# Second moments of 64-channel groups: one 128-column product per chunk half, or two 64-column products in the two halves of the array's columns

## The chip, the cores and the metric

The kernel runs on one core of one Trainium2 chip. The metric is the time of one execution on the device, in microseconds (us); lower is better. All tensors are float32.

The names used for the engines are those of the profile: PE is TensorE's matrix products and PEld its loads of weights (the stationary operand), DVE is VectorE, ACT is ScalarE, POOL is GpSimd, SP is SyncE, which here only issues DMAs.

## The reference

Two layers. The first computes 49 attention weights for every pixel from a dilated 7x7 convolution, a 1x1 convolution and a softmax, and sums the 49 shifted inputs with these weights. The second whitens the result in groups of 64 channels, and this is where the second moments come from:

```python
def _L1_conv_ref(X, weight, bias):
    NUM_CHANNELS = 64
    ...
    nc = NUM_CHANNELS
    g = C // nc
    x = jnp.transpose(X, (1, 0, 2, 3)).reshape(g, nc, -1)
    m = x.shape[-1]
    mean = x.mean(-1, keepdims=True)
    xc = x - mean
    I = jnp.broadcast_to(jnp.eye(nc, dtype=X.dtype), (g, nc, nc))
    Sigma = EPS * I + jnp.einsum('gdm,gem->gde', xc, xc) / m
    rTr = (1.0 / jnp.einsum('gii->g', Sigma))[:, None, None]
    Sigma_N = Sigma * rTr
    P = I
    for _ in range(T_ITERS):
        P3 = jnp.einsum('gij,gjk,gkl->gil', P, P, P)
        P = 1.5 * P - 0.5 * jnp.einsum('gij,gjk->gik', P3, Sigma_N)
    wm = P * jnp.sqrt(rTr)
    xn = jnp.einsum('gde,gem->gdm', wm, xc)
    X_hat = jnp.transpose(xn.reshape(C, B, H, W), (1, 0, 2, 3))
    return X_hat * weight + bias
```

The input is 4 images of 256 channels and 64x64 pixels, so there are four groups of 64 channels, and only the 64x64 blocks on the diagonal of the channel-by-channel moments are wanted.

## The kernel before

**Layout.** Channels lie on the partitions, 128 at a time (`NCC` = 2 halves, index `cc`). An image is split by the parity of rows and columns into four phases, so there are 16 phases `n` in all, and a phase is cut into 8 chunks of 128 pixels. Two phases share a slot in SBUF; the attention's result overwrites the input there.

**The convolution.** It is a fast algorithm with 7 evaluation points in each direction. `conv_bank` (L411, products at L430) multiplies a 49-column stationary operand with a moving operand of 128 or 162 columns; the inner loop `h` puts the two column phases into the partitions from 0 and from 64 of the same PSUM bank, so that it uses the array's columns in two halves. A row of evaluation points takes 104 products.

**The attention.** `softmax` (L565) turns the logits by the array (L571), takes the softmax on DVE and ACT, and stores the weights from the tile `zt` to DRAM by 8 DMAs of SP (L607). `load_band` (L616) reads them back skewed (L619), DVE transposes them into `band` (L630), `make_block` (L638) transposes a chunk of the input (L644, copied out at L651), and `weighted_sum` (L662) multiplies it with pieces of `band` of 64 to 352 columns (L676). `store_y` writes the result to the slot with ACT (L690).

**The second moments.** For each of the 128 chunks, `turn_y` (L700) transposes the result (two 128x128 products at L705) and ACT copies it from PSUM into one of three tiles `yt` (L712), which hold 128 channels and a column of ones for each half. `moments` (L714) then multiplies, for each half, the 128 channels as stationary operand with the 129 columns as moving operand (L718), and adds all chunks up in the PSUM tile `sig`: 128 columns of products and one column of sums. Of each 128x128 block the two off-diagonal quarters belong to no group; L877 sets them to zero with the mask `blk` at the end.

**The end.** After the last chunk, DVE forms the means `mu` (L866) and the scaled moments `S` (L872) from `sig`, a chain of small products gives the whitening matrices (L868 to L922), and a last pass multiplies all pixels with them (L937) and stores the output.

**What sets the order.** PE executes its products in the order of the program text, since `pe` keeps them so; the other engines' orders are made by a scheduler when the program is built. Of the eight calls of `moments` in a phase, four lie in `second_half` (L778) and four in `finish` (L746). Around them lie transposes (L644, L705) and weighted sums (L676); the call for chunk 3 is followed by the next step of the convolution wherever one is left. The convolution of image b+1 runs beside the attention of image b, so PE alternates between the two.

Of the kernel before, what the change touches and what calls it, by code (L numbers as in the profile page):

```python
# [8 lines left out]
F32 = mybir.dt.float32  # L9
AF = mybir.ActivationFunctionType  # L10
ALU = mybir.AluOpType
# [19 lines left out]
def kernel(  # L31
# [29 lines left out]
    nc = tc.nc  # L61
    B, C, H, W = x.shape
    P = 128
    NCC = C // P
# [6 lines left out]
    NCH = SH // CR  # L71
    HALF = SH // 2
    NPIX = B * H * W
    GW = 64
# [18 lines left out]
    def pe(ins):  # L93
        return tc.keep_in_program_order(ins)
# [7 lines left out]
    ps_sg = ctx.enter_context(tc.tile_pool(name="ps_sg", bufs=1, space=bass.MemoryType.PSUM))  # L102

    def tp():
        return ps_tp.tile([P, 512], F32, tag="tp", name="tp")
# [50 lines left out]
    t = tp()  # L156
# [3 lines left out]
    t = tp()  # L160
# [5 lines left out]
    for k in range(2):  # L166
        t = ps_cv.tile([P, 512], F32, name=f"cv{k}")
        nc.vector.memset(t, 0.0)
        cv_buf.append(t)
    sig = ps_sg.tile([P, NCC, P + 1], F32, name="sig")  # L170

# [366 lines left out]
    bpool = ctx.enter_context(tc.tile_pool(name="bp", bufs=1, side="right"))  # L540
# [5 lines left out]
    NY = 3  # L546
    yt_buf = []
    for k in range(NY):
        a = bpool.tile([P, NCC, P + 1], F32, name=f"yt{k}")
        nc.gpsimd.memset(a, 1.0)  # L550
        yt_buf.append(a)
    sd = []
    ND = SH + 2 * R
    for k in range(4):
        t = dram.tile([ND * DR], F32, name=f"sd{k}")
# [78 lines left out]
    def where(n):  # L634

        return slots[n // 2], n % 2
# [60 lines left out]
    count = [0]  # L697
    ybs = {}

    def turn_y(n, i):  # L700
        yt, pc = where(n)
        t = tp()
        for cc in range(NCC):
            pe(
                nc.tensor.transpose(  # L705
                    t[:, cc * P : (cc + 1) * P],
                    yt[:, cc, CR * i : CR * (i + 1), bass.ds(pc, SW, 2)],
                    ident,
                )
            )  # L710
        yb = ybs[n, i] = yt_buf[len(ybs) % NY]
        nc.scalar.copy(yb[:, :, :P], t[:, :C].rearrange("p (a c) -> p a c", a=NCC))  # L712

    def moments(n, i):  # L714
        yb = ybs[n, i]
        for cc in range(NCC):
            pe(
                nc.tensor.matmul(  # L718
                    sig[:, cc],
                    yb[:, cc, :P],  # L720
                    yb[:, cc, :],
                    start=(count[0] == 0 and cc == 0),
                    stop=(count[0] == 4 * B * NCH - 1),
                    skip_group_check=True,
                )
            )
        count[0] += 1

    spill = {}
# [16 lines left out]
    def finish(last=True):  # L746

        n = open_n[0]
        turn_y(n, 4)
        turn_y(n, 5)  # L750
        moments(n, 4)
        turn_y(n, 6)
        moments(n, 5)
        turn_y(n, 7)
        moments(n, 6)
        if n % 2:
            move(n // 2)
        if last:
            moments(open_n.pop(), 7)
# [90 lines left out]
    for k in range(3):  # L850
        t = rpool.tile([P, NCC, SH, W], F32, name=f"back{k}")
# [7 lines left out]
    def square(name):  # L859
        return bpool.tile([P, P], F32, tag="xb", name=name, bufs=5)  # L860

    wm, sc, beta = [], [], []
    for cc in range(NCC):
        G = sig[:, cc]
        mu = work.tile([P, 1], F32, tag="mu", name=f"mu{cc}")
        nc.vector.tensor_scalar(mu, G[:, P : P + 1], 1.0 / NPIX, None, ALU.mult)  # L866
        t = tp()
        nc.tensor.matmul(t[:1, :P], mu, ident, start=True, stop=True)  # L868
        row = work.tile([1, P], F32, tag="row", name=f"row{cc}", bufs=1)
        nc.vector.tensor_copy(row, t[:1, :P])  # L870
        S = work.tile([P, P], F32, tag="S", name=f"S{cc}")
        nc.vector.tensor_scalar(S, G[:, :P], 1.0 / NPIX, None, ALU.mult)  # L872
        t = tp()
        nc.tensor.matmul(t[:, :P], row, row, start=True, stop=True)
        nc.vector.tensor_tensor(S, S, t[:, :P], ALU.subtract)
        nc.vector.scalar_tensor_tensor(S, ident, EPS, S, ALU.mult, ALU.add)
        nc.vector.tensor_tensor(S, S, blk, ALU.mult)  # L877
        dt_ = square(f"dt{cc}")
        nc.vector.tensor_tensor(dt_, S, ident, ALU.mult)
        dg = work.tile([P, 1], F32, tag="dg", name=f"dg{cc}")  # L880
        nc.vector.tensor_reduce(dg, dt_, AX.X, ALU.add)
        t = tp()
        nc.tensor.matmul(t[:, :1], blk, dg, start=True, stop=True)
        rtr = work.tile([P, 1], F32, tag="rtr", name=f"rtr{cc}")
        nc.vector.reciprocal(rtr, t[:, :1])
        nc.vector.tensor_scalar(S, S, rtr, None, ALU.mult)


        Pm = square(f"P{cc}_0")
        nc.vector.tensor_scalar(Pm, ident, 1.5, None, ALU.mult)  # L890
        nc.vector.scalar_tensor_tensor(Pm, S, -0.5, Pm, ALU.mult, ALU.add)
        for it in range(1, T_ITERS):
            t = tp()
            nc.tensor.matmul(t[:, :P], Pm, Pm, start=True, stop=True)
            P2 = square(f"P2_{cc}_{it}")
            nc.vector.tensor_copy(P2, t[:, :P])
            t = tp()
            nc.tensor.matmul(t[:, :P], P2, Pm, start=True, stop=True)  # L898
            P3 = square(f"P3_{cc}_{it}")
            nc.vector.tensor_copy(P3, t[:, :P])  # L900
            t = tp()
            nc.tensor.matmul(t[:, :P], P3, S, start=True, stop=True)  # L902
            Pn = square(f"P{cc}_{it}")
            nc.vector.tensor_scalar(Pn, Pm, 1.5, None, ALU.mult)
            nc.vector.scalar_tensor_tensor(Pn, t[:, :P], -0.5, Pn, ALU.mult, ALU.add)
            Pm = Pn


        q = work.tile([P, 1], F32, tag="q", name=f"q{cc}")
        nc.scalar.activation(q, rtr, AF.Sqrt)  # L910
        qi = work.tile([P, 1], F32, tag="qi", name=f"qi{cc}")
        nc.vector.reciprocal(qi, q)
        nc.vector.scalar_tensor_tensor(q, qi, rtr, q, ALU.mult, ALU.add)
        scale = work.tile([P, 1], F32, tag="scale", name=f"scale{cc}")
        nc.vector.scalar_tensor_tensor(
            scale, q, 0.5, gain_sb[:, cc : cc + 1], ALU.mult, ALU.mult
        )
        t = tp()
        nc.tensor.matmul(t[:, :1], Pm, mu, start=True, stop=True)
        bt = work.tile([P, 1], F32, tag="beta", name=f"beta{cc}")  # L920
        nc.vector.tensor_scalar(bt, t[:, :1], scale, -1.0, ALU.mult, ALU.mult)
        nc.vector.tensor_tensor(bt, bt, shift_sb[:, cc : cc + 1], ALU.add)  # L922
        wm.append(Pm)
        sc.append(scale)
        beta.append(bt)
# [5 lines left out]
    for b in (3, 2, 1, 0):  # L931
        for cc in range(NCC):
            for q in range(SH // TR):
                st = rpool.tile([P, TR, 2, W], F32, tag="out", name=f"out_{b}_{cc}_{q}", bufs=4)
                for pr in range(2):
                    t = tp()
# [6 lines left out]
                        start=True,  # L943
                        stop=True,
# [46 lines left out]
```

## Time and profile before

| | us |
|---|---|
| median of 3 runs | 991.78 |
| lowest and highest of them | 989.21, 992.46 |
| the profiled execution | 991.09 |
| its span, first to last instruction | 989.3 |
| PE busy in the span | 793.0 |
| PEld busy | 694.3 |
| DVE busy | 660.3 |
| ACT busy | 305.2 |

The spans of busy time of different engines overlap. A float32 product appears in the trace as two weight loads and two matrix products, so the 256 products of `moments` are 512 records on PE and 512 on PEld. [...] what counts in a dense stretch is the distance from start to start. The first moments come at 301.0 us, the last at 887.2 us of the span.

### The profile page before, as it was taken

Reading aid. Unit: us, or ns where it says so; the run is one execution under the profiler, and the core shown is the slowest. Engines: PE = TensorE matmul, PEld = TensorE weight load, DVE = VectorE, ACT = ScalarE, POOL = GpSimd, SP = SyncE. Lnnn points to the kernel's source line nnn. Section 1 sums busy time; section 2 is a strip of 40 time slices with the busy share of each in tenths; the row PEclk is TensorE's granted clock in tenths of the full one; section 3 lists DMA queues with packets and bytes.
Section 4 is the critical chain, followed back from the end, with each engine's and each line's share of the span. In section 5 each row is a group of like instructions: output and inputs, shape, how many; then the busy total and the mean of one; then the engine's idle time right before and its main releaser. Section 6 shows DMA issues by size and latency. Waiting matters only on the chain.

```text
span 989.3 us, 19053 instructions
## 1 busy us (share of the span) xinstructions
PE 793.0 (80%) x7739; PEld 694.3 (70%) x7739; DVE 660.3 (67%) x1469; ACT 305.2 (31%) x654; POOL 38.1 (4%) x50
## 2 busy tenths in 40 slices
PE   5995575752679999894999989589997678885898
PEld 5995575752668889794888979578896557663443
DVE  3006999999996885998489589979567311113344
ACT  1214222331223333332243434213323323330143
POOL 2102000030000010001001000000000000000000
PEclk9988787877779999997899999989998879995699
DMA  9737221136575363269718223953214972200277
GB/s 277 176 64 190 89 71 62 55 106 230 97 154 127 109 186 90 59 171 192 155 46 247 74 66 86 166 119 100 56 45 132 246 116 51 48 0 1 85 309 286
DMA packets 189711, 122.09 MB, mean 123 GB/s; under 512 B 139655, under 2 KB 180664, under 8 KB 188600
## 3 DMA queue, kind: packets, MB, share of 16 engines
q1 hardware_dynamic: 184600, 90.73, 36.7%
q0 software_dynamic: 5024, 30.15, 9.9%
q8 instruction: 61, 1.00, 0.4%
q14 instruction: 26, 0.21, 0.1%
HBM read 69.64 MB, written 51.21 MB: 122 GB/s over the span
## 4 chain that ended last, share of the span: by engine, by line
PE 52%; DVE 9%; ACT 4%; DMA 3%; SPq 3%; issue 3%; DVEq 0%; ACTq 0%
PE cv L430 20%; PE y L676 15%; PE tp L937 6%; PE sig L718 4%; SPq L607 2%; PE tp L644 2%; DMA band<-sd 2%; PE tp L705 2%; DVE band L630 1%; DVE pv L282 1%; ACT slot L690 1%; ACT pv L439 1%; DVE zz L282 1%; PE tp L898 1%; PE tp L902 1%
## 5 line engine op out<-in xcount | busy, mean ns | idle before, releaser
L430 PE MATMUL cv<-xh,wr 128*49 128x128 f32 (+1 forms) x5408 | 335.3, 287 | 61.7 <-DVE xh L275 50.3
L430 PEld LDWEIGHTS cv<-xh,wr 128*49 128x49 f32 x5408 | 324.1, 128 | 69.8 <-issue 63.8
L676 PE MATMUL y<-band,xb 128*128 128x352 f32 (+5 forms) x768 | 178.1, 375 | 62.0 <-DVE band L630 45.5
L676 PEld LDWEIGHTS y<-band,xb 128*128 128x128 f32 x768 | 124.4, 206 | 82.2 <-issue 40.8
L630 DVE STREAM_TRANSPOSE band<-band 128x1408 f32<-128x1408 f32 x32 | 50.6, 1619 | 60.8 <-DMA band<-sd 60.8
L718 PE MATMUL sig<-yt 128*128 128x129 f32 x512 | 82.1, 283 | 11.2 <-ACT yt L712 11.1
L651 ACT COPY xb<-tp 128x256 f32<-128x256 f32 x128 | 46.0, 373 | 129.8 <-PE tp L644 129.5
L718 PEld LDWEIGHTS sig<-yt 128*128 128x128 f32 x512 | 71.3, 195 | 17.3 <-ACT yt L712 14.6
L439 ACT COPY pv<-cv 113x486 f32<-113x486 f32 (+1 forms) x84 | 39.8, 474 | 116.2 <-PE cv L430 113.4
L690 ACT ACTIVATE slot<-y,pivot 128x512 f32<-128x512 f32 x64 | 42.5, 721 | 64.3 <-PE y L676 64.3
L705 PE MATMUL tp<-ident,slot 128*128 128x128 f32 x256 | 52.9, 299 | 10.0 <-ACT slot L690 9.0
L282 DVE SCALAR_TENSOR_TENSOR xh<-ct 128x512 f32<-128x512 f32 x56 | 36.7, 683 | 30.2 <-PE cv L430 30.2
L712 ACT COPY yt<-tp 128x256 f32<-128x256 f32 x128 | 45.2, 378 | 33.7 <-PE tp L705 33.5
L644 PEld LDWEIGHTS tp<-ident,slot 128*128 128x128 f32 x256 | 44.3, 205 | 15.2 <-issue 6.3
L644 PE MATMUL tp<-ident,slot 128*128 128x128 f32 x256 | 52.7, 303 | 2.3 <-DVE d L581 2.3
L275 DVE TENSOR_TENSOR ct<-rb 128x1024 f32<-128x1024 f32 x28 | 33.9, 1211 | 29.8 <-ACT rb L361 29.6
L705 PEld LDWEIGHTS tp<-ident,slot 128*128 128x128 f32 x256 | 39.4, 204 | 17.4 <-ACT slot L690 14.0
L282 DVE SCALAR_TENSOR_TENSOR pv<-pv 113x162 f32<-113x162 f32 x168 | 49.0, 318 | 0.1
L233 PE MATMUL tp<-w2c,w 128*128 128x245 f32 x196 | 47.6, 409 | 0.0
L952 DVE TENSOR_SCALAR out<-tp,scale,beta 128x512 f32<-128x512 f32 x32 | 25.9, 810 | 32.5 <-PE tp L937 32.5
L233 PEld LDWEIGHTS tp<-w2c,w 128*128 128x128 f32 x196 | 45.7, 314 | 1.4
L282 DVE SCALAR_TENSOR_TENSOR xh<-rb 128x512 f32<-128x512 f32 x28 | 19.2, 686 | 37.5 <-PE cv L430 37.5
(152 smaller groups left out, 899.8 us busy)
## 6 DMA issues: line engine op xcount, KB each, us to landing
wr<-gd SPq DMA_DIRECT2D x108, 196.0 KB, 2.7
out_dram<-out SPq DMA_DIRECT2D x32, 512.0 KB, 2.6
sd<-zt SPq DMA_DIRECT2D x128, 112.0 KB, 2.8
band<-sd SPq DMA_DIRECT2D x64, 224.0 KB, 4.0
slot<-in_x_dram POOLq DMA_DIRECT2D x12, 1024.0 KB, 12.0
gd<-wr SPq DMA_DIRECT2D x36, 196.0 KB, 2.0
w<-in_L_conv_w_dram SPq DMA_DIRECT2D x2, 3136.0 KB, 12.1
spill<-slot POOLq DMA_DIRECT2D x3, 2048.0 KB, 10.4
```

What stands on the lines that cost most here:

```text
L233: nc.tensor.matmul(t[:, : MID * KT], tap(cc, a, s, v), w2c[:, a].rearrange("p b k -> p (b k)"), start=(a == 0), stop=(a == na - 1),)
L282: return STT(o, a, f, b, ALU.mult, ALU.add)
L430: nc.tensor.matmul(cv[h * HB : h * HB + KT, k, sr : sr + n, sc : sc + n], wv[:, sc, sr, cc], xh[bc][:, :n, h * NCC + cc, :n], start=(j == ...
L439: nc.scalar.copy(pvs[b, br][:K2, i0 : i0 + len(pts)].rearrange("p n q b -> p (n q b)"), cv[:K2, : len(pts)].rearrange("p n q b two -> p (n ...
L630: nc.vector.transpose(f, f)
L644: nc.tensor.transpose(t[:, cc * P : (cc + 1) * P], xt[:, cc, CR * m : CR * (m + 1), bass.ds(pc, SW, 2)], ident,)
L651: nc.scalar.copy(xb, t[:, :C])
L676: nc.tensor.matmul(ps[:, cc, q0 - half * HALF : q1 - half * HALF, :], xb[:, cc * P : (cc + 1) * P], rhs, start=(k == 0), stop=(k == len(PI ...
L690: nc.scalar.activation(yt[:, cc, half * HALF : (half + 1) * HALF, bass.ds(pc, SW, 2)], ps[:, cc], AF.Identity, bias=pivot[:, cc : cc + 1],)
L705: nc.tensor.transpose(t[:, cc * P : (cc + 1) * P], yt[:, cc, CR * i : CR * (i + 1), bass.ds(pc, SW, 2)], ident,)
L718: nc.tensor.matmul(sig[:, cc], yb[:, cc, :P], yb[:, cc, :], start=(count[0] == 0 and cc == 0), stop=(count[0] == 4 * B * NCH - 1), skip_gr ...
L937: nc.tensor.matmul(t, wm[cc], slots[2 * b + pr][:, cc, q * TR : (q + 1) * TR, :].rearrange("p r w -> p (r w)"), start=True, stop=True,)
```

## The change

Each product of `moments` over 128 channels becomes two, one for each group of 64. A group's 64 channels are the stationary operand, and the same 64 channels with their own column of ones are the moving operand (65 columns). The first group's result goes to partitions 0 to 63 of `sig`, the second's to 64 to 127, in the same columns, so the two products use the two halves of the array's columns. `sig` and `yt` get the shapes that this needs, `turn_y` copies four runs of 64 channels instead of two of 128, and at the end `S` is cleared and its two diagonal blocks are filled one by one.

```diff
-    sig = ps_sg.tile([P, NCC, P + 1], F32, name="sig")
+    sig = ps_sg.tile([P, NCC, GW + 1], F32, name="sig")
...
-        a = bpool.tile([P, NCC, P + 1], F32, name=f"yt{k}")
+        a = bpool.tile([P, NCC, P // GW, GW + 1], F32, name=f"yt{k}")
...
-        nc.scalar.copy(yb[:, :, :P], t[:, :C].rearrange("p (a c) -> p a c", a=NCC))
+        nc.scalar.copy(
+            yb.rearrange("p a g c -> p (a g) c")[:, :, :GW],
+            t[:, :C].rearrange("p (e c) -> p e c", c=GW),
+        )
...
         for cc in range(NCC):
-            pe(
-                nc.tensor.matmul(
-                    sig[:, cc],
-                    yb[:, cc, :P],
-                    yb[:, cc, :],
-                    start=(count[0] == 0 and cc == 0),
-                    stop=(count[0] == 4 * B * NCH - 1),
-                    skip_group_check=True,
+            for g in range(P // GW):
+                pe(
+                    nc.tensor.matmul(
+                        sig[g * GW : (g + 1) * GW, cc],
+                        yb[:, cc, g, :GW],
+                        yb[:, cc, g],
+                        start=(count[0] == 0 and cc == 0),
+                        stop=(count[0] == 4 * B * NCH - 1),
+                        skip_group_check=True,
+                    )
                 )
-            )
...
-        nc.vector.tensor_scalar(mu, G[:, P : P + 1], 1.0 / NPIX, None, ALU.mult)
+        nc.vector.tensor_scalar(mu, G[:, GW : GW + 1], 1.0 / NPIX, None, ALU.mult)
...
-        nc.vector.tensor_scalar(S, G[:, :P], 1.0 / NPIX, None, ALU.mult)
+        nc.vector.memset(S, 0.0)
+        for g in range(P // GW):
+            gs = slice(g * GW, (g + 1) * GW)
+            nc.vector.tensor_scalar(S[gs, gs], G[gs, :GW], 1.0 / NPIX, None, ALU.mult)
```

In the built programs, the order of PE's instructions is the same but for the products of `moments`: four products in place of two for each chunk. On the other engines the scheduler moved a few neighbours past each other. Two of them lie near DMAs: in the third and fourth image, SP's load of the convolution weights of row 1, bank 5 (L297) stands behind the first eight stores of attention weights (L607) instead of ahead of them. The two clearings of `S` stand at the very start of DVE's order.

## The prediction

> **What bounds the kernel now.** I read the page first (busy shares, then the chain that ended last), then the groups by form, then the chain in ten windows between 295 and 900 us, where all moments lie, and last the timeline of PE around single calls of `moments`.
>
> ```profile
> PE 793.0 (80%) x7739; PEld 694.3 (70%) x7739; DVE 660.3 (67%) x1469; ACT 305.2 (31%) x654; POOL 38.1 (4%) x50
> ...
> PE 52%; DVE 9%; ACT 4%; DMA 3%; SPq 3%; issue 3%; DVEq 0%; ACTq 0%
> PE cv L430 20%; PE y L676 15%; PE tp L937 6%; PE sig L718 4%; SPq L607 2%; PE tp L644 2%; DMA band<-sd 2%; PE tp L705 2%; DVE band L630 1%; DVE pv L282 1%; ACT slot L690 1%; ACT pv L439 1%; DVE zz L282 1%; PE tp L898 1%; PE tp L902 1%
> ```
>
> PE is the busiest engine and carries most of the chain. L718, the moments, has 4% of it. In the ten windows I counted 92 chain pieces of L718, 41 us in all, which are 93 of the 128 calls. So what a call gains or loses on PE shows in the end for some 7 calls in 10; the others lie where PE afterwards waits for ACT (L690) or for `band`.
>
> ```profile
> L430 PEld LDWEIGHTS cv<-xh,wr 128*49 128x49 f32 x5408 | 324.1, 128 | 69.8 <-issue 63.8 <-ACT pv L439 1.1
> L430 PE MATMUL cv<-xh,wr 128*49 128x128 f32 x4624 | 305.4, 282 | 0.0
> ...
> L718 PE MATMUL sig<-yt 128*128 128x129 f32 x512 | 82.1, 283 | 11.2 <-ACT yt L712 11.1
> L718 PEld LDWEIGHTS sig<-yt 128*128 128x128 f32 x512 | 71.3, 195 | 17.3 <-ACT yt L712 14.6
> ```
>
> The convolution, L430, is the model for the new products: it already puts 49-column weights into the two halves of the columns. Its 5408 records fill little more than 300 us, although one lasts 282 ns: they overlap. The timeline gives the distances:
>
> ```profile
> 425.83 12.14 PE L430 MATMUL cv<-xh,wr 128*49 128x162 f32 x208
> ```
>
> ```profile
> 484.52 1.24 PE L676 MATMUL y<-band,xb 128*128 128x320 f32 x4
> 485.60 0.61 PE L718 MATMUL sig<-yt 128*128 128x129 f32 x4
> 486.14 1.04 PE L430 MATMUL cv<-xh,wr 128*49 128x162 f32 x14
> ```
>
> ```profile
> 498.00 0.28 PE L430 MATMUL cv<-xh,wr 128*49 128x128 f32 x2
> ...
> 498.21 0.75 PE L705 MATMUL tp<-ident,slot 128*128 128x128 f32 x4
> ...
> 500.56 0.61 PE L718 MATMUL sig<-yt 128*128 128x129 f32 x4
> ...
> 501.01 0.40 PE L705 MATMUL tp<-ident,slot 128*128 128x128 f32 x2
> ...
> 501.74 0.64 PE L644 MATMUL tp<-ident,slot 128*128 128x128 f32 x4
> ```
>
> Columns: start in us, length in us, engine, line, operation, and how many records were merged. Four things are to be seen. (1) A call between full-width products takes 501.01 - 500.56 = 0.45 us: four records, 0.112 each. (2) The convolution's 208 records take 12.14 us, less 0.28 for the last one's passage, so a pair of records takes 11.86 / 104 = 0.114 us: two halves for the price of one full-width record. (3) Before a convolution the same call takes 486.14 - 485.60 = 0.54, so going from full width into halves costs 0.09. (4) Coming back, the first transposes start 0.21 after the last pair, whose own stream takes 0.11: 0.10 lost; and the four of them then take 0.75 where they take 0.64 in a dense stretch (501.74): another 0.11, a full-width weight load that could not be made ahead.
>
> [...] In the trace a full-width load follows the last at 0.11[...]. [...]
>
> **The change, part by part.**
>
> *The stream of a call.* Before: 4 records at 0.112, 0.45 us. After: 8 records, 4 pairs. A pair's columns are 65 instead of 129, and its weights 64 instead of 128, so it should take half of 0.112: 0.056; 4 x 0.057 = 0.23. A gain of 0.22. Bounds: with pairs that overlap imperfectly, five slots instead of four, 0.29; with no overlap at all (64 columns per load, one after the other) 0.45, no gain. I take 0.23, since L430's pairs do overlap.
>
> *The switches.* Before, a call lies in full-width work. Now it begins with a switch into halves, 0.09, and its first weight load of 64 columns is exposed, 0.05. It ends with a switch back. No row shows that for 65 columns: the loss is 0.10 if it begins when the stream ends, and 0.15 if the 0.21 from start to start is fixed (0.21 - 0.06). I take 0.12. Then the next product's full-width load is exposed, 0.11 (498.21 against 501.74). Sum: 0.37 lost, 0.22 gained: a call with full-width neighbours is longer by 0.15 (0.12 to 0.18).
>
> *By neighbours, on the chain.* I took each call's predecessor and successor from the timeline. 61 of the 93 have full-width work right before and after: 61 x 0.145 = +8.8 us. Ten go over into the convolution: there the switch existed, and it only moves to the call's front; the exit is free. Eight of them gain the 0.22 and lose nothing but a little weight load, 8 x -0.20 = -1.6; two also begin after a wait, [...] the exposed load shrinks from 0.11 to 0.05: 2 x -0.40 = -0.8. Eight others begin after a wait for `yt` (L712) and end in full-width work: 0.11 + 0.45 before, 0.05 + 0.23 + 0.12 + 0.11 after, -0.05 each, -0.4. The rest are calls that wait inside for `yt` (33 calls are stretched so, by 0.05 to 0.10); the longer call before them eats that wait: about eight on the chain, -0.5.
>
> *Off the chain.* 32 of the other 35 calls lie between full-width products, + 4.6 us of PE time there. It is covered by PE's waits, such as the half microsecond before L705 that waits for ACT L690. A fifth may come through: +1.0 (0 to 3).
>
> *SP's order.* In images 3 and 4 a weight load of the convolution no longer stands ahead of eight stores.
>
> ```profile
> 438.01 0.32 SPq L297
> ...
> 438.38 0.43 SPq L607
> ```
>
> That load waits for the end of the convolution (438.0), and the stores behind it are on the chain. `zt` was written by 437.90 (L598, 437.34 and 0.56 long), so they can start 0.4 earlier: 2 x -0.4 = -0.9 with its issue. The load itself is needed only at 486, and comes out at about 444.
>
> *Small edits.* The `yt` copy moves the same 128x256 in four runs; L651's contiguous one takes 373 ns, this one with two runs 378, so 5 ns more at most. The two clearings of `S` lie at the start of DVE, under PE's wait for weights (7 us); without that cover 0.3 us. Two fills of 64 columns instead of one of 128 (280 ns) stand in DVE's queue ahead of the second `mu`, and partly ahead of nothing that is waited for: the row copy (L870, 888.27) waits for PE anyway. Zero, at most 0.2. DVE's and ACT's other swaps: between -1 and +2, taken as 0.
>
> Sum: 8.8 - 1.6 - 0.8 - 0.4 - 0.5 + 1.0 - 0.9 = +5.6 us. On the profiled execution's own 991.09 that is 996.7; the median is 0.7 above it, so 997.
>
> **Rivals.**
>
> *No overlap of the short pairs.* Each call loses 0.22 more: the gain is gone and the switches stay. About 80 chain calls x 0.22 = +18: 1015. For it: the pair is so short that each half's load and stream have to fit into 0.056 us, and nothing in this trace is that short. Against: L430's pairs start together everywhere. 0.08.
>
> *The switches are mostly absorbed.* If the exit costs 0.10 and a longer call eats more of the `yt` and ACT waits than I counted, a call loses 0.10 and some 15 of the 61 vanish: +2 in sum, 994. For it: DVE and SP hold a good part of the chain between 430 and 470 and again from 620 to 650. Against: the second half of a phase is PE back to back. 0.22.
>
> *No switch at all, faster.* If what I read as a switch belongs to the convolution alone (its semaphores, its 162-column start), 64-column products flow between full-width ones, and each of the 93 calls saves 0.22: -20 us, 971. Place: entry and exit of `moments`. The point is 0.22 us for both together; below it the change gains. For it: all switches in this trace have the convolution on one side. Against: the entry into L430 costs the same 0.09 after L718 and after L676, the exit the same 0.10 before L644 and L705, whose weights lie ready in both cases. 0.08, together with smaller gains by luck of the order.
>
> **How the numbers follow.** The forecast has 0.62. Its own range: the exit (-1.5 to +1.8), five slots for four (+4.5), off the chain (-1 to +2), the other engines' order (-1 to +2): 994 to 1004. A measurement of this kernel tells about 0.3% from no change, 3 us. The absorbed case lies within it, as does the low end of my own; the case without overlap adds to slower. Slower 0.71, within 0.3% 0.20, faster 0.09. With half of the absorbed case taken in, the range is 992 to 1005.
>
> **What would show it.** In the profile after: L722, the new products, with 1024 records; a call from first start to the next product's start near 0.39 with 0.23 of it in four pairs (a pair near 0.057); the transposes behind it 0.1 longer; calls before the convolution shorter by 0.2; PE's busy time nearly the same; L718's 4% of the chain not smaller. The stores of `zt` in images 3 and 4 should no longer follow the load at the convolution's end. I am wrong if a call with its switches takes less than 0.45, or if PE's added time doesn't reach the chain.

## The result, and the profile after

| | before | changed |
|---|---|---|
| median, us | 990.5 (4 runs) | 995.79 (4 runs) |
| lowest and highest, us | 988.54, 992.46 | 995.47, 996.29 |
| profiled execution, us | 991.09 | 996.29 |
| span of it, us | 989.3 | 994.5 |

The ratio of changed to before is 1.0054, 95% interval 1.003 to 1.0078: slower by 5.3 us (3.0 to 7.7). The forecast was 997, 0.5% above the 991.78 that was the median of before then.

The page of the changed kernel, its busy line and its chain:

```profile
PE 801.3 (81%) x8251; PEld 677.6 (68%) x8251; DVE 661.4 (67%) x1473; ACT 305.3 (31%) x654; POOL 38.1 (4%) x50
...
PE 52%; DVE 9%; ACT 4%; DMA 3%; SPq 3%; issue 3%; DVEq 0%; ACTq 0%
PE cv L430 19%; PE y L676 16%; PE tp L944 6%; PE sig L722 3%; PE tp L705 3%; SPq L607 3%; PE tp L644 2%; DMA band<-sd 2%; DVE band L630 1%; ACT slot L690 1%; ACT pv L439 1%; DVE pv L282 1%; DMA sd<-zt 1%; DVE zz L282 1%; DVE xh L282 1%
```

The costliest groups of the changed kernel (busy us, mean ns of one, idle time before):

```profile
L705 PE MATMUL tp<-ident,slot 128*128 128x128 f32 x256 | 59.2, 324 | 10.2 <-ACT slot L690 9.3
L722 PE MATMUL sig<-yt 128*64 128x65 f32 x1024 | 58.2, 235 | 9.4 <-ACT yt L712 8.9
```

The same transposes in the kernel before:

```profile
L705 PE MATMUL tp<-ident,slot 128*128 128x128 f32 x256 | 52.9, 299 | 10.0 <-ACT slot L690 9.0
```

The moments themselves became cheaper: L722 is busy for 58.2 us where L718 was for 82.1, and its share of the chain falls from 4% to 3%. But the transposes behind them, L705, rose from 52.9 to 59.2 us although their code is the same, and all of PE from 793.0 to 801.3. Each single call shows it. The timeline of PE around two calls between full-width work, that is, between products that use all 128 columns of the array (start, length, engine, line, operation, records merged):

```profile
500.37 0.45 PE L722 MATMUL sig<-yt 128*64 128x65 f32 x8
500.76 0.51 PE L705 MATMUL tp<-ident,slot 128*128 128x128 f32 x2
501.19 0.45 PE L722 MATMUL sig<-yt 128*64 128x65 f32 x8
501.57 0.74 PE L644 MATMUL tp<-ident,slot 128*128 128x128 f32 x4
```

The same place in the kernel before:

```profile
500.33 0.40 PE L705 MATMUL tp<-ident,slot 128*128 128x128 f32 x2
500.56 0.61 PE L718 MATMUL sig<-yt 128*128 128x129 f32 x4
501.01 0.40 PE L705 MATMUL tp<-ident,slot 128*128 128x128 f32 x2
501.25 0.66 PE L718 MATMUL sig<-yt 128*128 128x129 f32 x4
```

And the changed kernel around the call ahead of a convolution:

```profile
484.41 1.34 PE L676 MATMUL y<-band,xb 128*128 128x320 f32 x4
485.68 0.45 PE L722 MATMUL sig<-yt 128*64 128x65 f32 x8
485.96 1.22 PE L430 MATMUL cv<-xh,wr 128*49 128x162 f32 x18
```

From first start to the next product's start a call takes 500.76 - 500.37 = 0.39 us, 0.06 less than before. Against this, the two transposes take 0.51 instead of 0.40, and the call starts 501.19 - 500.76 = 0.43 after them where it started 0.24 after (501.01 and 501.25). From one call to the next the kernel before repeats every 0.69 us (500.56 to 501.25), the changed one every 0.82 (500.37 to 501.19): 0.13 longer. Ahead of a convolution the call takes 0.28 instead of 0.54. The weight loads show where a part of this lies: before, they start 0.11 to 0.12 us ahead of their product (500.90 for the transposes at 501.01, 500.44 for the call at 500.56); in the changed kernel those of the call start with it, both at 500.37, and those of the transposes behind it at 500.75 and 500.76. A load that starts with its product is the exposed load of the prediction.

### The profile page after: what moved, and what is told of

Its sections match the earlier page's. It is cut to its first block, busy times and chain, and to the rows that moved or that the text cites. A ratio compares the mean times of both kernels' runs of the same rounds, so it can differ in the third digit from the quotient of the medians.

```text
span 994.5 us, 20076 instructions
## 1 busy us (share of the span) xinstructions
PE 801.3 (81%) x8251; PEld 677.6 (68%) x8251; DVE 661.4 (67%) x1473; ACT 305.3 (31%) x654; POOL 38.1 (4%) x50
## 4 chain that ended last, share of the span: by engine, by line
PE 52%; DVE 9%; ACT 4%; DMA 3%; SPq 3%; issue 3%; DVEq 0%; ACTq 0%
PE cv L430 19%; PE y L676 16%; PE tp L944 6%; PE sig L722 3%; PE tp L705 3%; SPq L607 3%; PE tp L644 2%; DMA band<-sd 2%; DVE band L630 1%; ACT slot L690 1%; ACT pv L439 1%; DVE pv L282 1%; DMA sd<-zt 1%; DVE zz L282 1%; DVE xh L282 1%
## 5 line engine op out<-in xcount | busy, mean ns | idle before, releaser
L676 PE MATMUL y<-band,xb 128*128 128x352 f32 (+5 forms) x768 | 183.1, 382 | 64.7 <-DVE band L630 47.2
L676 PEld LDWEIGHTS y<-band,xb 128*128 128x128 f32 x768 | 125.7, 207 | 86.6 <-DVE band L630 37.1
L705 PE MATMUL tp<-ident,slot 128*128 128x128 f32 x256 | 59.2, 324 | 10.2 <-ACT slot L690 9.3
L722 PE MATMUL sig<-yt 128*64 128x65 f32 x1024 | 58.2, 235 | 9.4 <-ACT yt L712 8.9
L722 PEld LDWEIGHTS sig<-yt 128*64 128x64 f32 x1024 | 40.4, 137 | 33.7 <-ACT yt L712 13.2
L644 PE MATMUL tp<-ident,slot 128*128 128x128 f32 x256 | 55.5, 314 | 0.0
L705 PEld LDWEIGHTS tp<-ident,slot 128*128 128x128 f32 x256 | 39.1, 206 | 21.7 <-ACT slot L690 14.0
```

The source lines that it names most:

```text
L644: nc.tensor.transpose(t[:, cc * P : (cc + 1) * P], xt[:, cc, CR * m : CR * (m + 1), bass.ds(pc, SW, 2)], ident,)
L676: nc.tensor.matmul(ps[:, cc, q0 - half * HALF : q1 - half * HALF, :], xb[:, cc * P : (cc + 1) * P], rhs, start=(k == 0), stop=(k == len(PI ...
L705: nc.tensor.transpose(t[:, cc * P : (cc + 1) * P], yt[:, cc, CR * i : CR * (i + 1), bass.ds(pc, SW, 2)], ident,)
L722: nc.tensor.matmul(sig[g * GW : (g + 1) * GW, cc], yb[:, cc, g, :GW], yb[:, cc, g], start=(count[0] == 0 and cc == 0), stop=(count[0] == 4 ...
```

## The experiments

Each was run beside the kernel before on the same chip, whose median there was 991.8 to 992.1 us.

| run | median, us | ratio to before, 95% interval |
|---|---|---|
| e1 full width, small edits kept | 990.91 | 0.9989 (0.9977 to 1.0001) |
| e2 before, one load on POOL | 989.1 | 0.9972 (0.9963 to 0.998) |
| e3 halves, four calls together | 980.7 | 0.9893 (0.9874 to 0.9912) |
| e4 full width, four calls together | 990.53 | 0.9992 (0.9978 to 1.0006) |
| e5 before, an extra visit to the halves | 1017.27 | 1.0259 (1.0245 to 1.0273) |
| e6 changed, loops swapped | 996.5 | 1.0045 (1.0031 to 1.0059) |
| e7 changed, the same load on POOL | 998.49 | 1.0065 (1.0052 to 1.0079) |
| e8 halves, batch ahead of the sum | 980.51 | 0.9883 (0.9867 to 0.99) |
| e9 full width, batch ahead of the sum | 988.11 | 0.9963 (0.9949 to 0.9978) |

**e1: only the halves undone.**

```diff
-            for g in range(P // GW):
-                ... sig[g * GW : (g + 1) * GW, cc], yb[:, cc, g, :GW], yb[:, cc, g]
+            ... sig[:, cc], yb[:, cc, :P], yb[:, cc, :]
...
-            nc.vector.tensor_scalar(S[gs, gs], G[gs, :GW], 1.0 / NPIX, None, ALU.mult)
+            nc.vector.tensor_scalar(S[gs, gs], G[gs, gs], 1.0 / NPIX, None, ALU.mult)
```

> The change without its halves: products of 128 by 129 columns as before, but the copy into yt in four runs, S cleared and filled block by block, and mu from column 128. Theory (the halves and their switches make the loss): as the kernel before, 988 to 993 us. Rival (the small edits make it: the copy, the fills of S): as the changed kernel, 994 us or more.

990.91 us, no difference from before. The four-run copy, the cleared `S` and its two fills cost nothing that can be measured; the loss comes with the 64-column products and with what the scheduler made of them.

**e5: a visit to the halves by itself.** Two 64x65 products, whose results nothing reads, stand ahead of each call of the kernel before.

```diff
+        for g in range(P // GW):
+            pe(nc.tensor.matmul(extra[g * GW : (g + 1) * GW],
+                                yb[:, 0, g * GW : (g + 1) * GW], yb[:, 0, : GW + 1], ...))
         for cc in range(NCC):
```

> The kernel before, with two 64 by 65 products in the column halves put ahead of each call of moments, into unused columns of the bank of sig; nothing is taken away. It measures a visit to the halves by itself. Theory: entry 0.09, exposed load 0.05, two pairs 0.12, exit 0.09 beyond the stream, exposed full-width load 0.10: 0.45 us a visit, for some 93 calls on the chain 40 us: 1028 to 1034. Rival (the switch belongs to the convolution alone): two pairs only, 0.12 x 93 = 11: 1003.

The timeline of PE in e5 around one such call (L707 are the transposes, L720 the extra products, L731 the moments):

```profile
511.26 0.40 PE L707 MATMUL tp<-ident,slot 128*128 128x128 f32 x2
511.59 0.34 PE L720 MATMUL sig<-yt 128*64 128x65 f32 x4
511.86 0.71 PE L731 MATMUL sig<-yt 128*128 128x129 f32 x4
512.41 0.40 PE L707 MATMUL tp<-ident,slot 128*128 128x128 f32 x2
```

From transposes to transposes it is 1.15 us where it was 0.68 (500.33 to 501.01), so a visit costs 0.47 us: the price was right (0.45 expected), and the convolution has no part in it. But the whole is 25 us longer, not 36 to 42. A part of the reason is found in the weighted sums, below.

**e3 and e4: four calls together.** The four calls of a half phase are made at its end, with six `yt` tiles, so that four calls share the switches; e4 does the same with the full-width products.

```diff
-    NY = 3
+    NY = 6
...
+    def four(n, h):
+        for i in range(4 * h, 4 * h + 4):
+            moments(n, i)
...
-        moments(n, 0)
...
-        moments(n, 3)
+        four(n, 0)
```

> The changed products, but the four calls of moments of a half phase together at its end (six yt tiles in place of three), so that there is one entry into halves and at most one exit per four calls. Theory (stream 0.23 us a call, 0.14 for the entry, 0.23 to 0.26 for the exit, free where a convolution follows): 32 batches of 1.06 plus some 16 exits make 38 us of PE where before has 58, some 70% of it on the chain: 977 us, 972 to 984, faster than both kernels. Rival (the short pairs bring nothing that shows): not below 988.

> The same batching with the full-width products of before: what the moving alone does. Theory: the products take as long as before, so 990 us, give or take 5 for transposes that now wait for their copies with less to fill the wait; 10 to 18 us above the batched halves. Rival (batching itself is the gain): within 3 us of the batched halves.

A batch of e3 on PE, and the same batch in e4:

```profile
480.35 1.15 PE L722 MATMUL sig<-yt 128*64 128x65 f32 x32
481.33 1.44 PE L430 MATMUL cv<-xh,wr 128*49 128x162 f32 x21
```

```profile
482.37 1.95 PE L718 MATMUL sig<-yt 128*128 128x129 f32 x16
484.25 2.98 PE L430 MATMUL cv<-xh,wr 128*49 128x162 f32 x48
```

The busy lines of their pages, e3 first:

```profile
PE 772.8 (79%) x8251; PEld 667.9 (68%) x8251; DVE 661.8 (68%) x1473; ACT 300.7 (31%) x654; POOL 38.9 (4%) x53
```

```profile
PE 794.0 (80%) x7739; PEld 694.3 (70%) x7739; DVE 660.6 (67%) x1469; ACT 300.6 (30%) x654; POOL 38.9 (4%) x53
```

Four calls take 481.33 - 480.35 = 0.98 us in halves and 484.25 - 482.37 = 1.88 in full width. This batch goes over into the convolution; where full-width work follows, a batch in halves takes 1.08. e3 is 11 us faster than before and some 15 us faster than the changed kernel, with the same 64-column products; e4, with the same moves, is no faster than before. So the products in halves are worth having, and what made the change lose is the number of visits: one for each call.

SP's order is not the same in all of these: e3 has that of the changed kernel, and e4 has one load more behind the stores, so what e3 gains over the kernel before can hold something of the 2.8 us of e2, below. e8 and e9, further below, both have the order of the kernel before, and there the halves are 7.6 us ahead.

**e6: the loops swapped.**

```diff
-        for cc in range(NCC):
-            for g in range(P // GW):
+        for g in range(P // GW):
+            for cc in range(NCC):
```

> The changed kernel with its two loops swapped: both halves of the channels for the first group, then both for the second, so that products of the same columns follow each other. If only products in different columns overlap: a call's stream is three slots of a single record longer or more, 0.06 to 0.22 us, 5 to 18 us in all: 1001 to 1014. If the array takes records as they come, two at a time: as the changed kernel, 996.

996.5 us, as the changed kernel. A call on PE in e6, and then one in the changed kernel:

```profile
300.93 0.46 PE L722 MATMUL sig<-yt 128*64 128x65 f32 x8
301.31 0.51 PE L705 MATMUL tp<-ident,slot 128*128 128x128 f32 x2
```

```profile
301.37 0.45 PE L722 MATMUL sig<-yt 128*64 128x65 f32 x8
301.76 0.51 PE L705 MATMUL tp<-ident,slot 128*128 128x128 f32 x2
```

0.38 against 0.39 here, and 0.390 against 0.383 in the mean of the calls between full-width work: the products of the two halves need not alternate in the program. In the trace the records still start in pairs, only 13 ns apart instead of 7. A record does not name its half, so which two run side by side is not shown.

**e2 and e7: SP's order.** The load of the convolution weights of row 1, bank 5 in images 3 and 4 is issued by POOL, in the kernel before (e2) and in the changed one (e7), so that SP's order is the same in the two.

```diff
-                nc.sync.dma_start(w[bc], gd[br]...)
+                q = nc.gpsimd if (b > 1 and br == 1 and i == 2) else nc.sync
+                q.dma_start(w[bc], gd[br]...)
```

> The kernel before, with only the load of weights of row 1, bank 5 in images 3 and 4 issued by POOL, so that SP's stores of attention weights need not stand behind it. The prediction took 0.9 us for the same move in the changed kernel: 989.6 us. The trace after points to more: the drift against before falls by some 2 us at each of the two places, which would give 986 to 987. If the drift falls for another reason, no change: 990.5.

> The changed kernel with the load of row 1, bank 5 in images 3 and 4 issued by POOL, as in the run of before with it there. With SP's order the same in both, what stays between the two is the moments. Theory (the order hid part of what the halves cost): as the changed kernel, 995 to 997, so 6 to 8 us above the kernel before with the load on POOL (989.1). Rival (the order has no part): 993, the same 3 us lower as before was.

e2 is faster by 2.8 us (2.0 to 3.7), three times what I had taken for this order and less than the 3.5 to 4.5 that I then read from the trace. In the changed kernel, which has it by the scheduler, the chain of waits at the first of the two places reads:

```profile
438.64 0.48 DVE zt L598
439.12 0.12 DVE s L590
439.24 0.28 SPq L607
```

The stores (L607) now follow the tile that they store (L598). Before, they followed the load (L297), which follows the convolution's end on PE. That cuts PE's delay off from them: measured by the starts of the same products, the changed kernel is 2.1 us behind at 428 and 0.8 behind at 469, where the next weighted sum starts; at the second place it goes from 2.5 behind at 607 to 0.7 behind at 648. (It is 0.3 ahead at 481, but the rest of that is the sum itself, which ran at a higher granted clock than before, 0.74 against 0.63.) I had priced the wait (0.4 us each), not that PE's lost time no longer runs through this chain. With the order the same in both, e7 stands 1.0065 / 0.9972 = 0.93% above e2, 9 us (7 to 12 by the ends of the two intervals): that is what the 64-column products bring, with all that they set off. It is not their price alone: in the two profiled executions, 7.8 us apart, 2.8 us arise between 619 and 648 us, where only four calls lie. What causes that is not shown. e7 itself came out at 998.5, neither at 995 to 997 nor at 993; its interval and that of the changed kernel overlap.

**The weighted sums and the granted clock.** The 24 records of a phase's first weighted sum (L676, with the transposes between them) take 4.8 us from the first start to the last in some phases and 6.3 to 7.8 in others, in every kernel. Three windows, each around the same sum, of before, of the changed kernel and of e5 (columns: us, busy us and records of PE, PEld, DVE, ACT, POOL, granted clock, DMA share, GB/s):

```profile
844.90:849.90 5.00, 4.95 (x28) 4.25 (x29) 1.48 (x1) 0.74 (x2) 0.00 (x0) 1.00 0.00 0
```

```profile
848.00:854.60 6.60, 6.52 (x28) 5.11 (x29) 1.51 (x1) 0.74 (x2) 0.00 (x0) 0.74 0.01 2
```

```profile
871.10:876.00 4.90, 4.89 (x28) 4.16 (x29) 1.43 (x1) 0.74 (x2) 0.00 (x0) 1.00 0.01 3
```

The same 28 records of PE, and only the granted clock differs: 1.00, 0.74, 1.00. The 0.74 is a mean: in the changed kernel's window the clock is 1.00 from 848.0 to 848.7, 0.50 from 848.8 to 852.1 and 1.00 from 852.2 to 854.6. Ahead of the sum PE waits 2.10 us before and 2.19 in the changed kernel, for `band`, and 0.92 in e5, whose extra work fills most of the wait. Over all eleven kernels, sums after a wait of up to 1.8 us took at most 4.9 us; after 3.3 us or more, at least 6.3. In between both occur, and not by length. These two sums, of e7 and then of e9, had a clock of 0.75 and of 1.00 (idle time before, and what ended it, in brackets; L677 of e7 is L676 of the others):

```profile
875.17 2.54 PE L677 MATMUL y<-band,xb 128*128 128x352 f32 x4 [1.95 <-DVE band L631]
```

```profile
846.01 1.45 PE L676 MATMUL y<-band,xb 128*128 128x352 f32 x4 [3.19 <-DVE band L630]
```

So long waits go with a lower clock, but between 1.9 and 3.2 us the length of this one wait does not decide it; what else does is not shown. Added up over the 16 sums of each profiled execution: 95.3 us before, 98.9 changed, 100.4 in e3, 100.5 in e4, 86.5 in e5. So the sums of e5 gave back 9 us, where it fell 11 to 17 short of what was expected; how much of that lay on the chain is not taken apart. e3 lost 5, but this is not why a saving of PE time of 20 us (793.0 to 772.8) brought only 11: e4 lost as much, and is 21 us of PE time and only 10 us of time above e3. About half of the saved PE time lies where the end does not wait for it; which part is not shown.

**e8 and e9: the batch put into the wait.** If it is the wait that lowers the clock, which was my guess from these sums, a batch ahead of the first sum, which fills the wait, should keep it up.

```diff
         make_block(n, 3)
+        if open_n:
+            four(open_n.pop(), 1)
         weighted_sum(n, 0, 0)
...
         store_y(n, 0)
-        if open_n:
-            four(open_n.pop(), 1)
```

> Batches of four calls in halves as in e3, but the batch of chunks 4 to 7 stands just ahead of the next phase's first weighted sum, where PE waits for band, in place of behind it. Theory (a wait of 2 us or more ahead of these sums lets the granted clock fall, and the sum takes 6.5 us instead of 4.85; and work in the wait costs nothing): some of the 16 first sums return to 4.85, and part of the batches, 1.06 us each and 0.23 for the exit, lies in the waits: 972 us, 966 to 979. Rival (the clock has nothing to do with the wait): as e3, 979 to 983.

> The same places with the full-width products of before. In the waits the batch of 1.8 us is as free as the short one and fills more of the wait; only the batches at the end of the second half, 16 of them, differ by 0.87 to 0.65 us: 982 us, 976 to 988, so 6 to 14 above the halves. If the halves brought nothing here: within 3 us of each other.

e8 is no better than e3: 980.5 us, not 966 to 979. That is the time that was named for the rival, in which the clock has nothing to do with the wait. But its trace shows the waits only shortened, not filled: its batch of 1 us shortens the last three waits of the span from 4.3, 4.4 and 4.5 us to 3.3, 3.4 and 3.6, behind which no sum here took less than 6.3, and all 16 sums together still take 100.1 us. In e9, with batches of 1.8 us, two sums after waits of 1.98 and 1.99 us are at 4.87, which in e4 stood behind 3.78 us each and took 6.54 and 7.50, and the 16 take 89.7 us. So the link between wait and clock rests on e5 and e9, neither of which changes the wait alone. e9 came out at 988.1, the upper end of what was expected, 3.7 us under before; that this comes from the sums and the hidden batches is likely but not separated. The halves are 7.6 us ahead of the full width here. e3 and e8 stay the fastest, 11 us under before.

## Why the prediction was right

The direction and the size came out, and the step that carried them, a short product between two switches, is shown by the trace and by e5. That the sum came so near is in part luck, as two of its terms were off in opposite directions (below). Term by term, us of one call (from the start of the record before to the second record after; ahead of a convolution, to its second pair):

| | predicted | measured |
|---|---|---|
| stream of four pairs | 0.23 (0.057 a pair) | 0.23 to 0.24 (0.059 a pair) |
| entry | 0.09 | 0.09 |
| exposed half-width load at the front | 0.05 | 0.05 (0.108 from the first pair to the second) |
| last pair to the next full-width start | 0.15 to 0.21 | 0.15 |
| exposed full-width load behind | 0.11 | 0.10 |
| call between full-width work | +0.145 | +0.13 |
| call ahead of a convolution | -0.20 | -0.20 |
| call behind a wait | -0.05 | -0.06 |
| both | -0.40 | -0.40 |

*The convolution as a model* was right: pairs of half the columns follow each other at about half the full-width distance (0.059 us against 0.112), and the extra distances at the switches and the exposed full-width load could be read from its borders. The 0.05 for an exposed load of 64 columns was an estimate, no reading of the trace, and about half of the 0.11 of a full-width load; the first two pairs of a call, 0.108 apart where the others are 0.059, agree with it. Two readings of it were a little off, without effect: 28 of the 208 records behind the 0.114 have 162 columns, and pairs of 128 alone are 0.111 apart; and its records fill 335 us, not little more than 300. The open end was the exit, and its lower value holds: the distance follows the stream (0.15 us behind 65 columns, 0.21 behind 128).

*The sum.* On the calls of the chain I had 8.8 - 1.6 - 0.8 - 0.4 - 0.5 = +5.5; the same calls, measured one by one, give about +3.9. The 61 cost 0.11 on the mean rather than 0.145: the exit was cheaper, and calls that used to wait inside for `yt` lost that wait.

*Two terms were mis-sized, in opposite directions.* SP's order brought 2.8 us (e2), not 0.9. And the products cost more than the 6.5 that I had for them on and off the chain: 9 us in e7 against e2. The other 35 calls add about 3.3 us of PE time, so all 128 calls make about 7; the 9 us is as much or more, so most of what I had put off the chain seems to come through, and what is above 7 is not explained. The two errors are about 2 and 3 us, and the sum is nearer than its parts. How much came through in the changed kernel itself stays open, since the clock moved there too.

*The clock* was no term of mine. In the profiled pair the first sums are 3.6 us longer, and one sum that had stayed at full clock before (the one of the three windows above) gives 1.7 of the 5.2 us between the two executions, so that this pair comes so near the forecast is luck as well. It is not peculiar to the change: the profiled executions of e7 and e2 differ by 7.8 us with equal sums, 95.1 and 95.3.

*The rivals.* No overlap (1015): out, by the 0.059 of a pair. No switch outside the convolution (971): out, by e5. Mostly absorbed (994): the time alone doesn't exclude it (3.0 to 7.7 us slower), and its grounds came true in part: the exit loses 0.09 beyond the stream, and a call loses 0.11 in the mean. But that the rest is absorbed is out, by the 9 us of e7 against e2; what hid a part of the loss was SP's order, which I had counted small.

*The signs I named.* 0.39 us a call (0.45 + 0.13 = 0.58 with its switches), transposes 0.1 longer, calls before the convolution shorter, the stores no longer behind the load: as said. PE's busy time rose by 8.3 us where I said nearly the same, and the moments' share of the chain fell to 3%, since the cost of the visit is booked on its neighbours.

## What to carry to other kernels

Price a product in column halves by the visit, not by the product: here a visit cost some 0.35 us at its entry and exit and in exposed loads (the 0.47 of e5 less two pairs of records at 0.059), and a call of two short-product pairs saved only 0.22. Gather enough work for one visit, or put it next to work that is in halves already (0.28 instead of 0.54 us for a call ahead of the convolution): with four calls in a visit the same products made the kernel 11 us faster. A look at the cost of an instruction's neighbours is part of its price, for the profile books a part of the switch on them (L705 here, 299 to 324 ns each).

When PE time saved and time saved differ, compare the same instructions' durations at both ends: the same 28 records took 4.95 us at a granted clock of 1.00 and 6.52 at 0.74 here, and slow sums mostly followed longer waits (in the kernel before, nine of the ten behind 2.1 us or more, none of the six behind 0.6 or less). In e3 and e4 alike the 16 sums took 5 us longer than before. And not all PE time saved shows: e3 has 21 us less of it than e4 and is only 10 us faster.

## What the runs showed of the hardware

- Leaving the halves: the next full-width product starts 0.15 us after the last pair of 65 columns (changed kernel), 0.21 after one of 128 (both kernels), about 0.09 to 0.10 beyond the pair's own 0.06 or 0.11.
- Entering the halves: 0.09 us more than the distance that full-width products keep, 0.20 instead of 0.11 behind 96 columns (both kernels) or 129 (before), 0.28 instead of 0.19 behind 224, 0.36 instead of 0.27 behind 320 (changed kernel).
- The products of the two halves need not alternate in the program: eight records with the four of one half first took 0.390 us in the mean (e6), and 0.383 with two and two (changed kernel).
- Waits of PE of about 2 us and the granted clock in the sum that follows: after 1.95 us a sum ran at 0.75 (e7), after 2.19 at 0.74 (changed kernel), after 2.10 at 1.00 (before) and after 3.19 at 1.00 (e9).
